# Four query products and four value-weight products of layer 1, held in written order on TensorE

## The chip, the cores and the metric

The kernel runs on one NeuronCore of a Trainium2 chip. Its time is the device time of one execution in microseconds (us). The kernel before took 3039.69 us as the median of 16 runs (3030.94 to 3050.21).

## The reference, cut to what matters

The reference is four transformer layers over 4 sequences of 512 tokens, 256 features each; every layer adds an attention-like part and a feed-forward part to `x`. Layer 1, where the change lies, is

```python
q = _rmsnorm(x @ wq_a, q_a_ln_w) @ wq_b            # 16 heads, 128 + 64 numbers each
q_nope, q_pe = q[..., :128], q[..., 128:]
ckv = x @ wkv_a
kv = _rmsnorm(ckv[..., :64], kv_a_ln_w) @ wkv_b    # per head: k_nope (128) and v (128)
q_pe, k_pe = _apply_rope(q_pe), _apply_rope(ckv[..., 64:])
scores = (q_nope @ k_nope.T + q_pe @ k_pe.T) * 192 ** -0.5     # causal
out = softmax(scores) @ v                          # all 16 heads side by side
x = x + out @ wo + _L1_ffn_ref(xn, ...)            # product-key experts and a gated unit
```

All of it is float32.

## The kernel before

**Absorbed weights.** The kernel never forms k_nope or v. Four times in layer 1, once for each group of four heads, `carry(g)` (L999 to L1022) multiplies the head's query weights by its key weights, `pw` (L1007) and `pw1` (L1015), and its value weights by its rows of `wo`, `pv` (L1008, the "value products"). ScalarE copies the results to SBUF (`wl0`, `wl1`, `wz`, L1019 to L1021). A value product has a stationary operand of 128 x 64, so it uses half of the columns of the array: heads 0 and 2 write partitions 0 to 63 of `pv`, heads 1 and 3 write partitions 64 to 127.

**Queries.** Heads go in pairs: 4 groups of heads, 4 sequences and 2 pairs make 32 pairs. For a pair, `queries(p)` (L1024 to L1046) makes two banks of 128 x 512 in PSUM, `pe` (the rotary part) and `pl` (the latent part). The contraction over 192 query latents is cut into 128 and 64, so each bank takes two matmuls: L1033 (`pe`, 128 rows), L1034 (`pl`, 128 rows), L1035 (`pe`, 64 rows: partitions 0 to 63) and L1036 (`pl`, 64 rows: partitions 64 to 127). In the text they are P0, L0, P1 and L1. P1 and L1 use different halves of the rows of the array. Every float32 matmul shows as two passes in the trace. Then ScalarE copies `pe` to `pes` (L1039), four SyncE DMAs swap 32-row blocks of it into `psw` (L1041), ScalarE scales `pl` into `qf` (L1043, L1044), and later VectorE rotates (`rotate`, L1048 to L1053) and writes the rest of `qf`.

**Heads.** The main loop (L1179 on) goes over 64 heads `s`. For each head, `probabilities(s, i)` for i = 0 to 3 makes the scores of query block i against keys 0 to 128(i+1) (L949, TensorE), adds the mask and takes the maximum (L952, VectorE), takes the exponential (L956, ScalarE), and, from i = 2 on, inverts the sums (L1067, VectorE) and multiplies by them (L1069, ScalarE: three tiles `pr0` to `pr2` after i = 2, the last, `pr3`, after i = 3). Beside it `turned(s - 1, j)` (L1071 to L1080) transposes column block j of the head before, 4 - j blocks of 128 x 128, on TensorE (L1076), and a copy of them to `PT` follows (L1080). Every second head, L1212 multiplies `PT` with the latents and L1226 with `wz`.

The next pair's queries are written after step i = 1 of every even head:

```python
            if i == 1 and s % 2 == 0 and s < 62:
                turning = queries(s // 2 + 1)
```

**What sets the order.** `weave` (L501) interleaves four streams of layer 1 by their costs: the attention, the product-key experts (L1236 on, mostly VectorE), a gated unit (L134, L212) and, at the end, the routing of layer 2. That gives the order in which instructions are *written*. The order in which they are *issued* is set afterwards: a scheduler at build time puts each engine's instructions in the order in which it reckons them ready, and keeps only true dependences. An engine then works through its list in that order. `tc.keep_in_program_order(ins)` adds one tie: `ins` is issued behind the instruction that was written just before it on the same engine, whichever stream that was. It adds no semaphore and no wait of its own; and something else may still be put between the two. The kernel before uses it in layer 1 for L1212, for L1051 and for the experts' dot products (L1340), not for the products of `queries` or `carry`.

Of the kernel before, what the change touches and what calls it, by code (L numbers as in the profile page):

```python
# [82 lines left out]
def v3(ap, b):  # L83
    return ap.rearrange("p (a b) -> p a b", b=b)
# [890 lines left out]
def latent_pieces(c, a, keep, open_pool):  # L975
# [4 lines left out]
    nc, tc = c.nc, c.tc  # L980
    QL, KL = 192, 64
# [3 lines left out]
    qa0 = c.tile(keep, [P, NT], "qa0")  # L985
    qa1 = c.tile(keep, [P, NT], "qa1")
# [12 lines left out]
    def carry(g):  # L999

        w = c.unit(a["l_units"][g])
        wqT, wkT, wvT = v3(w[:, :768], QL), v3(w[:, 768:1024], KL), v3(w[:, 1024:1280], KL)
        wo = v3(w[:, 1792:2816], DM)
        pw, pv = c.ps(), c.ps()
        for h in range(4):
            hk = slice(h * KL, (h + 1) * KL)
            nc.tensor.matmul(pw[:, hk], lhsT=wqT[:, h, :P], rhs=wkT[:, h, :], start=True, stop=True)  # L1007
            nc.tensor.matmul(  # L1008
                pv[(h % 2) * KL : (h % 2 + 1) * KL, (h // 2) * DM : (h // 2 + 1) * DM],
                lhsT=wvT[:, h, :], rhs=wo[:, h, :], start=True, stop=True,  # L1010
            )
        pw1 = c.ps()
        for h in range(4):
            hk = slice(h * KL, (h + 1) * KL)
            nc.tensor.matmul(pw1[KL:, hk], lhsT=wqT[:, h, P:], rhs=wkT[:, h, :], start=True, stop=True)  # L1015
        wl0 = c.tile(pool, [P, 256], "wl0")
        wl1 = c.tile(pool, [P, 256], "wl1")
        wz = c.tile(pool, [P, 2, DM], "wz")
        nc.scalar.copy(wl0, pw[:, :256])  # L1019
        nc.scalar.copy(wl1[KL:, :], pw1[KL:, :256])  # L1020
        nc.scalar.copy(wz, v3(pv, DM))  # L1021
        weights[g] = w[:, 1280:1536], w[:KL, 1536:1792], wl0, wl1, wz  # L1022

    def queries(p):  # L1024

        g, b, pair = p // 8, p // 2 % 4, p % 2
        if p % 8 == 0:
            carry(g)
        wpe0, wpe1, wl0, wl1, _ = weights[g]
        tokens = slice(b * SEQ, (b + 1) * SEQ)  # L1030
        cols = slice(pair * P, (pair + 1) * P)
        pe, pl = c.ps(), c.ps()
        nc.tensor.matmul(pe, lhsT=wpe0[:, cols], rhs=qa0[:, tokens], start=True, stop=False)  # L1033
        nc.tensor.matmul(pl, lhsT=wl0[:, cols], rhs=qa0[:, tokens], start=True, stop=False)  # L1034
        nc.tensor.matmul(pe, lhsT=wpe1[:, cols], rhs=qa1[:KL, tokens], start=False, stop=True)  # L1035
        nc.tensor.matmul(pl, lhsT=wl1[KL:, cols], rhs=qa1[KL:, tokens], start=False, stop=True)  # L1036

        pes, psw = (c.tile(pool, [P, SEQ], n, bufs=1) for n in ("pes", "psw"))
        nc.scalar.copy(pes, pe)  # L1039
        for to in range(0, P, 32):  # L1040
            nc.sync.dma_start(psw[to : to + 32, :], pes[to ^ 32 : (to ^ 32) + 32, :])  # L1041
        qf = c.tile(pool, [P, 2, SEQ], "qf")
        nc.scalar.mul(qf[:KL, 0, :], pl[:KL, :], -scale)  # L1043
        nc.scalar.mul(qf[KL:, 1, :], pl[KL:, :], -scale)  # L1044
        qfs[p] = qf
        return pes, psw, qf  # L1046
# [85 lines left out]
    for b in range(NB):  # L1132
        tokens = slice(b * SEQ, (b + 1) * SEQ)
        lats.append(latents(b))
        for t in range(TPB):
            tt = b * TPB + t
            pl = c.ps()[:, : QL + KL]
# [28 lines left out]
    finish(0)  # L1166
    yield 1.9
    turning = queries(0)
    yield 2.6
    finish(1)  # L1170
# [8 lines left out]
    for s in range(65):  # L1179
        if s < 64:  # L1180
            prs[s] = []
        for i in range(TPB):
            if s < 64:
                probabilities(s, i)
            if s > 0:
                if i == 0:
                    PTs[s - 1] = c.tile(pool, [P, 1280], "PT")
                ready, copy = copy, turned(s - 1, i)
                if ready:
                    ready()  # L1190
            if i == 0 and s % 2 == 1 and s < 63:
                rotate(*turning)
            yield 0.85
            if i == 1 and s % 2 == 0 and s < 62:
                turning = queries(s // 2 + 1)
                yield 2.6
# [13 lines left out]
        for j in range(TPB):  # L1210
            for h in range(2):
                tc.keep_in_program_order(nc.tensor.matmul(  # L1212
                    z[h * KL : (h + 1) * KL, j * P :], lhsT=cv[:, b * TPB + j, :],
                    rhs=PTs[s - 2 + h][:, START[j] : START[j] + SEQ - j * P],
                    start=(j == 0), stop=(j == TPB - 1),
# [4 lines left out]
        if pair == 1:  # L1220
            wz = weights[g][4]
            for t in range(0, TPB, 2):
                po = v3(c.ps("acc"), DM)
                for j in range(2):
                    for k in range(2):
                        nc.tensor.matmul(  # L1226
                            po[:, j, :], lhsT=zTs[k][:, (t + j) * P : (t + j + 1) * P],
                            rhs=wz[:, k, :], start=(k == 0), stop=(k == 1),
# [1078 lines left out]
```

## Time and profile before

| what | value |
|---|---|
| median of 16 runs | 3039.69 us |
| lowest, highest | 3030.94, 3050.21 us |
| the profiled execution: its own time | 3030.7 us |
| its span, first to last instruction | 3028.9 us |
| mean granted TensorE clock | 0.997 |
| TensorE busy | 2967.4 us (98% of the span) |
| VectorE, ScalarE, GpSimd busy | 2121.0 (70%), 1399.6 (46%), 915.6 us (30%) |

The profile is of one execution. "Busy" is the union of an engine's instructions; matmuls overlap in the pipeline and their ends are modelled, so what a matmul really takes of TensorE is read from the distance between the starts of two matmuls that follow each other. An "idle before" is only time in which no instruction of that engine ran. Layer 1's queries begin 836.5 us after the start of the span (first P0) and end at about 1444 us. The 16 runs lie in clusters: six at 3031, six at 3039 to 3041, four at 3044 to 3050; the profiled execution is one of the low ones.

### The profile page before, as it was taken

Reading aid. Unit: us, or ns where it says so; the run is one execution under the profiler, and the core shown is the slowest. Engines: PE = TensorE matmul, PEld = TensorE weight load, DVE = VectorE, ACT = ScalarE, POOL = GpSimd, SP = SyncE. Lnnn points to the kernel's source line nnn. Section 1 sums busy time; section 2 is a strip of 40 time slices with the busy share of each in tenths; the row PEclk is TensorE's granted clock in tenths of the full one; section 3 lists DMA queues with packets and bytes.
Section 4 is the critical chain, followed back from the end, with each engine's and each line's share of the span. In section 5 each row is a group of like instructions: output and inputs, shape, how many; then the busy total and the mean of one; then the engine's idle time right before and its main releaser. Section 6 shows DMA issues by size and latency. Waiting matters only on the chain.

```text
span 3028.9 us, 39747 instructions
## 1 busy us (share of the span) xinstructions
PE 2967.4 (98%) x13674; PEld 1957.4 (65%) x13674; DVE 2121.0 (70%) x5366; ACT 1399.6 (46%) x3336; POOL 915.6 (30%) x749
## 2 busy tenths in 40 slices
PE   8999999999999999999998999999999999999999
PEld 5666666566655555555676677777777756666666
DVE  5877878787777778787665767666666756666665
ACT  5444544444466666667524444444444433333332
POOL 0665555556210133332234200010010033333332
PEclk9999999999999999999999999999999999999999
DMA  3333333232221244444234000000000000000000
GB/s 134 94 108 123 98 97 117 83 124 84 88 69 37 64 120 105 104 104 123 83 105 127 16 1 29 1 22 8 1 21 1 22 1 22 22 22 22 22 1 29
DMA packets 89114, 185.39 MB, mean 61 GB/s; under 512 B 14192, under 2 KB 57216, under 8 KB 84176
## 3 DMA queue, kind: packets, MB, share of 16 engines
q1 hardware_dynamic: 74448, 135.05, 14.0%
q0 software_dynamic: 14176, 47.01, 6.6%
q8 instruction: 108, 1.77, 0.2%
q14 instruction: 94, 0.77, 0.1%
q10 hardware_dynamic: 288, 0.79, 0.1%
HBM read 160.92 MB, written 12.98 MB: 57 GB/s over the span
## 4 chain that ended last, share of the span: by engine, by line
PE 84%; DVE 8%; ACT 2%; DMA 2%; POOL 2%; issue 1%; SPq 0%; ACTq 0%; DVEq 0%; POOLq 0%
PE mm L301 19%; PE mm L134 14%; PE mm L949 7%; PE acc L301 6%; PE acc L1539 5%; PE acc L965 4%; PE tr L787 3%; PE tr L301 3%; PE tr L1531 2%; PE tr L1076 2%; PE mm L142 2%; PE tr L212 2%; PE acc L1212 2%; PE acc L765 2%; PE acc L212 2%; PE mm L1930 1%
## 5 line engine op out<-in xcount | busy, mean ns | idle before, releaser
L956 ACT ACTIVATE pr<-pr,nm 128x128 f32<-128x128 f32 (+3 forms) x512 | 286.3, 559 | 267.2 <-DVE nm L952 263.3
L312 ACT COPY part<-mm 128x256 f32<-128x256 f32 (+1 forms) x462 | 208.7, 459 | 232.1 <-PE mm L301 229.1
L301 PE MATMUL mm<-token_sums,unit_sums 128*128 128x512 f32 (+1 forms) x744 | 303.2, 490 | 0.0
L134 PE MATMUL mm<-xnT,wu 128*128 128x512 f32 x624 | 291.1, 604 | 3.8 <-DVE nm L952 3.7
L1330 POOL DMA_INDIRECT e<-in_p_experts,ids x128 | 128.9, 1007 | 478.0 <-DVE x L152 338.9
L952 DVE CUSTOM_DVE_ANT_0 pr<-mm,late 128x128 f32<-128x128 f32 (+3 forms) x512 | 245.6, 482 | 20.1 <-PE mm L949 17.3
L134 PE MATMUL mm<-xnT,w_in 128*128 128x512 f32 x512 | 229.2, 593 | 0.6 <-DVE cy L555 0.6
L461 DVE SCALAR_TENSOR_TENSOR x<-acc,cw,x 128x128 f32<-128x128 f32 x384 | 133.0, 347 | 112.4 <-PE acc L301 110.3
L134 PEld LDWEIGHTS mm<-xnT,wu 128*128 128x128 f32 x624 | 115.5, 192 | 125.4 <-issue 110.3
L555 DVE SCALAR_TENSOR_TENSOR cy<-mm,ws,cy 128x509 f32<-128x509 f32 (+2 forms) x216 | 160.2, 744 | 51.8 <-ACT cy L551 47.9
L949 PE MATMUL mm<-kf,qf 128*128 128x128 f32 (+3 forms) x512 | 176.0, 443 | 5.9 <-DVE qf L1053 4.5
L949 PE MATMUL mm<-k,q 128*128 128x128 f32 (+3 forms) x512 | 176.4, 434 | 1.1 <-DVE q L1478 1.0
L725 POOL TENSOR_TENSOR G<-G,CB 128x1024 f32<-128x1024 f32 x64 | 151.4, 2365 | 81.5 <-DVE G L688 75.4
L708 ACT ACTIVATE xD<-xc,ws 128x128 f32<-128x128 f32 x256 | 83.9, 391 | 191.7 <-POOL y L749 182.4
L301 PEld LDWEIGHTS acc<-down_sums,hidden_sums 128*128 128x128 f32 x768 | 114.8, 191 | 86.6 <-issue 83.4
L1532 DVE COPY PT<-tr 128x512 f32<-128x512 f32 (+3 forms) x256 | 124.7, 487 | 60.4 <-PE tr L1531 58.5
L134 PEld LDWEIGHTS mm<-xnT,w_in 128*128 128x128 f32 x512 | 96.5, 190 | 104.4 <-issue 94.4
L1539 PE MATMUL acc<-PT,V 128*128 128x512 f32 (+3 forms) x512 | 153.1, 442 | 7.3 <-DVE PT L1532 7.3
L688 DVE TENSOR_TENSOR_SCAN G<-G,eye 128x1024 f32<-128x1024 f32 x64 | 148.2, 2315 | 0.0
L1539 PEld LDWEIGHTS acc<-PT,V 128*128 128x128 f32 x512 | 93.3, 190 | 74.2 <-issue 30.6
L301 PE MATMUL mm<-xnT,wu 128*128 128x256 f32 (+1 forms) x368 | 137.0, 454 | 0.0
L444 DVE TENSOR_TENSOR whole<-mm,part 128x512 f32<-128x512 f32 x128 | 88.6, 692 | 68.2 <-PE mm L301 67.4
(408 smaller groups left out, 6713.9 us busy)
## 6 DMA issues: line engine op xcount, KB each, us to landing
G<-own SPq DMA_DIRECT2D x64, 512.0 KB, 4.4
w_in<-in_m_units SPq DMA_DIRECT2D x16, 1024.0 KB, 5.2
eb<-since SPq DMA_DIRECT2D x96, 128.0 KB, 3.3
wu<-in_o_units SPq DMA_DIRECT2D x8, 1536.0 KB, 6.5
wo<-in_m_units SPq DMA_DIRECT2D x16, 512.0 KB, 4.2
psw<-pes SPq DMA_DIRECT2D x128, 64.0 KB, 3.2
wu<-in_g_units SPq DMA_DIRECT2D x4, 1536.0 KB, 6.6
wu<-in_f_units SPq DMA_DIRECT2D x4, 1536.0 KB, 7.8
```

Source lines behind the costliest of these rows:

```text
L134: c.nc.tensor.matmul(out, lhsT=w[:, d, cols], rhs=c.xnT[:, d, tokens], start=(d == 0), stop=(d == 1))
L301: self.c.tc.keep_in_program_order(self.c.nc.tensor.matmul(bank, lhsT=lhsT, rhs=rhs, start=first, stop=True, skip_group_check=not first))
L312: self.c.nc.scalar.copy(r, bank)
L461: c.nc.vector.scalar_tensor_tensor(x, bank, self.factor(u, tt), x, ALU.mult, ALU.add)
L555: nc.vector.scalar_tensor_tensor(y[:, j:], src[:, : SEQ - j], conv[:, k, 3 - j : 4 - j], y[:, j:], ALU.mult, ALU.add,)
L688: tc.keep_in_program_order(nc.vector.tensor_tensor_scan(flat, flat, eye.rearrange("p h t -> p (h t)"), 0.0, ALU.mult, ALU.add))
L725: nc.gpsimd.tensor_mul(G, G, seqs[b][2][:, t, :][:, None, :].to_broadcast([P, HG, P]))
L949: kept(nc.tensor.matmul(sc, lhsT=q[:, i * P : n], rhs=k[:, :n], start=True, stop=True))
L952: nc.vector.tensor_tensor_reduce(out=pr, in0=sc, in1=late[:, SEQ - n :], scale=scale, scalar=-NEG, op0=ALU.add, op1=ALU.min, accum_out=nm,)
L956: nc.scalar.activation(pr, pr, AF.Exp, bias=nm, scale=-1.0, accum_out=total)
L1330: nc.gpsimd.indirect_dma_start(out=e, out_offset=None, in_=a["p_experts"], in_offset=bass.IndirectOffsetOnAxis(ap=ids[:, t, k : k + 1], ax ...
L1539: tc.keep_in_program_order(nc.tensor.matmul(z[:, j * P :], lhsT=head["V"][:, j, h, :], rhs=head["PT"][:, j, j * P :], start=(j == 0), stop ...
```

## The change

The four products of a pair and the four value products of a group are each passed through `keep_in_program_order`, and the value products get a loop of their own behind the loop of the query-key products. No instruction is added or taken away, and no size or operand is changed.

```diff
         for h in range(4):
             hk = slice(h * KL, (h + 1) * KL)
             nc.tensor.matmul(pw[:, hk], lhsT=wqT[:, h, :P], rhs=wkT[:, h, :], start=True, stop=True)
-            nc.tensor.matmul(
+        for h in range(4):
+            tc.keep_in_program_order(nc.tensor.matmul(
                 pv[(h % 2) * KL : (h % 2 + 1) * KL, (h // 2) * DM : (h // 2 + 1) * DM],
                 lhsT=wvT[:, h, :], rhs=wo[:, h, :], start=True, stop=True,
-            )
+            ))
...
-        nc.tensor.matmul(pe, lhsT=wpe0[:, cols], rhs=qa0[:, tokens], start=True, stop=False)
-        nc.tensor.matmul(pl, lhsT=wl0[:, cols], rhs=qa0[:, tokens], start=True, stop=False)
-        nc.tensor.matmul(pe, lhsT=wpe1[:, cols], rhs=qa1[:KL, tokens], start=False, stop=True)
-        nc.tensor.matmul(pl, lhsT=wl1[KL:, cols], rhs=qa1[KL:, tokens], start=False, stop=True)
+        kept, mm = tc.keep_in_program_order, nc.tensor.matmul
+        kept(mm(pe, lhsT=wpe0[:, cols], rhs=qa0[:, tokens], start=True, stop=False))
+        kept(mm(pl, lhsT=wl0[:, cols], rhs=qa0[:, tokens], start=True, stop=False))
+        kept(mm(pe, lhsT=wpe1[:, cols], rhs=qa1[:KL, tokens], start=False, stop=True))
+        kept(mm(pl, lhsT=wl1[KL:, cols], rhs=qa1[KL:, tokens], start=False, stop=True))
```

Lines behind the change stand one or two lines lower in the changed kernel (L1076 becomes L1078, L1033 to L1036 become L1035 to L1038 in written order).

## The prediction

> **What bounds the kernel.** I read the busy table and the chain of waits first. TensorE carries the end:
>
> ```profile
> PE 2967.4 (98%) x13674; PEld 1957.4 (65%) x13674; DVE 2121.0 (70%) x5366; ACT 1399.6 (46%) x3336; POOL 915.6 (30%) x749
> ...
> PE 84%; DVE 8%; ACT 2%; DMA 2%; POOL 2%; issue 1%; SPq 0%; ACTq 0%; DVEq 0%; POOLq 0%
> ```
>
> So time that TensorE gains or loses in layer 1 is, to first order, time of the kernel. Then TensorE's timeline at one group of products (group 4; I count the 32 pairs from 0). Columns: start, busy, line, number of passes.
>
> ```profile
> 906.15 1.02 PE L1033 MATMUL mm<-qa,wu 128*128 128x512 f32 x2
> 907.01 1.02 PE L1034 MATMUL mm<-qa,wl 128*128 128x512 f32 x2
> 907.99 0.84 PE L1076 MATMUL tr<-con,pr 128*128 128x128 f32 x3
> 908.76 1.12 PE L1035 MATMUL mm<-qa,wu 64*128 64x512 f32 x2
> 909.81 0.66 PE L1076 MATMUL tr<-con,pr 128*128 128x128 f32 x4
> 910.39 1.12 PE L1036 MATMUL mm<-qa,wl 64*128 64x512 f32 x2
> 911.45 1.13 PE L134 MATMUL mm<-xnT,wu 128*128 128x512 f32 x2
> ```
>
> Seven transposes of the head before (L1076) stand between the products. P1 (L1035) and L1 (L1036) take 1.05 us each (908.76 to 909.81). And here is a group that the scheduler left together (group 2):
>
> ```profile
> 871.65 1.02 PE L1033 MATMUL mm<-qa,wu 128*128 128x512 f32 x2
> 872.51 1.02 PE L1034 MATMUL mm<-qa,wl 128*128 128x512 f32 x2
> 873.46 0.69 PE L1035 MATMUL mm<-qa,wu 64*128 64x512 f32 x1
> 873.47 0.69 PE L1036 MATMUL mm<-qa,wl 64*128 64x512 f32 x1
> 874.00 0.59 PE L1035 MATMUL mm<-qa,wu 64*128 64x512 f32 x1
> 874.00 0.59 PE L1036 MATMUL mm<-qa,wl 64*128 64x512 f32 x1
> 874.52 0.91 PE L949 MATMUL mm<-kf,qf 128*128 128x384 f32 x2
> ```
>
> P1 and L1 start 0.007 us apart and run side by side: 1.06 us for both. The whole group takes 2.87 us.
>
> **What the change does to the order.** I compared the two programs' order on each engine. Before, P1 and L1 are neighbours in 13 of 32 groups, after it in 31 (not in group 0). But the tie reaches further: P0 is held behind whatever was written just before it, and that is the seven transposes. So in the changed program group 4 reads
>
> ```
> L1078 x7 (transposes), L1035 (P0), L1036 (L0), L1037 (P1), L1038 (L1)
> ```
>
> Seven transposes go ahead of the products, uncovered, in 15 of the 18 newly joined groups (3, 4, 5, 7, 12 to 15, 17, 18, 21, 23, 26, 29, 31). Outside layer 1 no engine's order changes.
>
> **Gain: sharing the array.** Group 15 is a split group with no visible wait: 4.83 us from P0 to the instruction after L1. Take off seven transposes at 0.109 us each (0.76, the distance of their starts) and 4.07 us are left, against 2.87: 1.20 us per group, of which 1.05 is the second 64-row product and 0.15 the slower starts around it. If nothing waited, 18 x 1.20 = 21.6 us. By the Trainium skill, "TensorE: Matmul & The Clock Gate", section "Measured speedup vs the span model", the second tile would cost only about 4 ns over the first; the rows show 0.53 us per shared pass, where a 128-row pass takes 0.43. By that rule a joined group would take 2.58 us, and the 18 would gain another 5 us; group 2 says no.
>
> **Gain: value products.** In groups of heads 1 and 3, L1007 and L1008 alternate; from 991.83 to 995.40 this takes 3.57 us. At 1146.00 two neighbouring L1008 products share the array: 0.58 us for both, where one alone takes 0.57. L1007 takes 0.22 us per head inside a run (start distances 0.11). New: 4 x 0.22 + 0.05 for the switch + 2 x 0.52 = 1.97, a gain of 1.6 us twice. Group of heads 2 has one shared pair already and group 0 is mixed with L1107's transposes; I take 0.8 for each (bounds 0 and 1.6). Together -4.8 us.
>
> **Loss: the transposes now wait uncovered.** This is the decisive step. What the seven transposes need comes from ScalarE:
>
> ```profile
> 906.83 0.72 ACT L956 ACTIVATE pr<-pr,nm 128x512 f32<-128x512 f32 x1 [0.35 <-DVE nm L952]
> 907.46 0.19 ACT L956 ACTIVATION_READ_ACCUMULATOR pr<-pr,nm 128x1 f32 x1
> 907.55 1.91 ACT L1069 ACTIVATE pr<-pr,total 128x128 f32<-128x128 f32 x4
> ```
>
> The four L1069 end at 907.94, 908.34, 908.85 and 909.46; the first transpose ran at 907.99, the second at 908.39, 0.05 us after their tile. TensorE was free at 906.15, and P0, L0 and P1 filled the time. ScalarE is not behind: it had idled 0.35 us for VectorE. This is the latency of score, mask, exponential, sum, scaling, and it won't move. In the changed order TensorE stands at 906.15 before a transpose that isn't ready until 907.99, and the last two can't run before 909.46 + 0.05. They end at 909.73 and the joined group at 912.60, against 911.45: **+1.15 us**, the 1.20 included.
>
> Generally: with R the end of the last L1069 after TensorE is free, the block takes R + 0.05 + 0.22 + 2.87. Over the 15 groups R is, in order, 3.00, 3.31, 3.06, 2.58, 3.94, 3.49, 2.94, 2.79, 3.38, 2.93, 2.57, 3.22, 3.04, 3.43, 2.21 (sum 45.9); the same instructions took 4.99, 5.30, 5.05, 4.97, 5.65, 5.77, 4.94, 4.83, 4.99, 4.92, 4.96, 4.99, 5.04, 4.89, 4.62 (sum 75.9). So 45.9 + 15 x 3.14 = 93.0 against 75.9: **+17.1 us**. The break-even is R = 5.06 - 3.14 = 1.9 us; the smallest is 2.21.
>
> The trace shows such a wait already. In group 6 the transposes stand ahead of the products, and no product passes them:
>
> ```profile
> 946.77 1.34 PE L1076 MATMUL tr<-con,pr 128*128 128x128 f32 x5 [0.70 <-ACT pr L1069]
> 948.29 0.44 PE L1076 MATMUL tr<-con,pr 128*128 128x128 f32 x2 [0.18 <-ACT pr L1069]
> ```
>
> Other groups, by the same reckoning: 16 (joined, transposes not moved) -1.15; 19 and 20 (L212 now covers the wait) -0.1 and -1.3; 10, 11 and 27 (joined before, now two or three transposes earlier) +1.4, +0.2, +0.4; 28 and 30 (layernorm's and seven other transposes go ahead) between 0 and +3.1 each, I take +1. Sum +1.5.
>
> **Who waits behind.** Behind a waiting transpose stand the products, then the next L949, whose scores VectorE (L952) waits for. `pe` of group 4 is complete at 912.60 instead of 909.81, so `pes`, the four SyncE DMAs (3.2 us to landing), `rotate` and `qf` come 2.8 us later, while their reader comes 1.15 later. VectorE's L1050 waits for `pes` with the experts' products queued behind it. TensorE's waits for `qf` are 4.5 us in three places now; if each grows by 1.6, +5. The other way, waits of up to 5 us on ScalarE and VectorE elsewhere can shrink while they catch up. I take +2 (-5 to +8). Moved SyncE issues (three) and one GpSimd copy: nothing, both queues are mostly empty.
>
> **Sum.** 17.1 + 1.5 - 4.8 + 2 = **+15.8 us**. On the profiled execution's own time, 3030.7, that is 3046.5. But that run is in the lowest of the clusters; the median stands 9.0 above it, so for a median I take 3039.7 + 15.8 = 3055.5, **3055 us**.
>
> **Rivals.**
> - *Nothing waits, faster.* If R fell below 1.9 us, blocks would shorten; at R under 0.5 the whole -21.6 - 4.8 = -26.4 us comes: 3013. For it: 98% busy, and the joined groups of before. Against it: R of 2.2 to 3.9 in all 15 groups, set by four L1069 in series. Chance 0.10.
> - *The wait is given back.* ScalarE and VectorE run ahead during each stop, and waits later in the pair vanish: the loss shrinks to within 6 us, 3034 to 3046. For it: VectorE is busy 79% between 940 and 1420 us (379.8 of 480), so it may profit. Against it: TensorE's listed waits in this stretch are only some 11 us. Chance 0.12.
> - *The stops also cost clock.* Between 1460 and 1480 us TensorE was busy 18.72 of 20 us, and the granted clock was 0.89: 2.2 us lost with 1.3 us idle. If a third of the 17 stops brought this, +12: 3068. "TensorE: Matmul & The Clock Gate", "Why this matters for your kernels", asks for no idle gap over about 3 us; gaps of under 2 us between transposes would cost nothing by it, but the row had less. Chance 0.10.
> - *Forecast*, +8 to +25 us: 0.68.
>
> **Range.** Low end: R shorter by 0.7 us in each block (-10.5) and the knock-on at -5 leave -2: 3037. High end: knock-on at +8 and groups 28 and 30 at their bound make +26, and a quarter of the stops losing clock brings 3074. Left out: the faster case and half of the clock case, near 0.16. What this kernel can tell from no change is 0.2%, 6.1 us: slower 0.78, same 0.12, faster 0.10.
>
> **What would show it.** In the new profile P1 and L1 start within 0.01 us of each other in 31 groups; L1078 (the transposes) shows idle time before it, released by ScalarE's scaling (now L1071), of some 15 x 2.5 = 38 us in place of 4.3; joined groups take 2.87 us; in layer 1 the span grows, before and behind it nothing moves. Wrong would be the step on R if those idle times stay under 1 us a group.

## The result and the profile after

The changed kernel takes 3094.69 us as the median of 11 runs (3087.93 to 3109.07), against 3040.65 us for the kernel before in the same comparison: ratio 1.0178 [1.0163, 1.0193], 54 us slower. The sign was forecast, the size was not: 3055 was predicted, and the range ended at 3074.

The profiled execution took 3090.85 us, 60.2 us more than that of before. First the busy table and the chain of waits of the changed kernel's page:

```profile
PE 2981.3 (97%) x13674; PEld 1959.9 (63%) x13674; DVE 2126.1 (69%) x5366; ACT 1398.7 (45%) x3336; POOL 912.9 (30%) x749
...
PE 80%; DVE 9%; ACT 4%; DMA 3%; POOL 2%; issue 1%; SPq 1%; DVEq 0%; ACTq 0%; POOLq 0%
```

TensorE has the same 13674 passes and is 14 us *more* busy, although products now share the array; ScalarE's part of the chain went from 2% to 4%. Where it lies is read by matching equal instructions of the two traces. Up to 836 us the changed kernel is 1.5 us late, at the last query product 56.7, at the end 60.2. So 55.9 of the 60.2 us lie between the first query product (P0) and the last (L1): this stretch takes 607.6 us before and 663.5 after. The windows over that stretch, before and then after (columns: window, its length, busy us of PE, PEld, DVE, ACT and POOL with their instructions, granted TensorE clock, DMA share, GB/s):

```profile
836.00:1445.00 609.00, 597.33 (x2627) 340.67 (x2626) 479.47 (x1657) 403.32 (x1066) 129.09 (x140) 1.00 0.36 90
```

```profile
836.00:1501.00 665.00, 608.86 (x2632) 342.40 (x2631) 484.93 (x1663) 402.74 (x1065) 128.03 (x143) 0.96 0.32 82
```

Two things are read off here. TensorE stood still for 609.00 - 597.33 = 11.7 us before and for 56.1 us after. And the granted clock fell from 1.00 to 0.96: the trace has 12 periods of half clock in this stretch, 51.2 us together, where before there was none.

Most of the idle time is the one that was predicted. The transposes' wait for the scaling in this stretch before (us in total, times, longest), and TensorE's waits after:

```profile
PE tr L1076 <- ACT pr L1069: 1.2, 4, 0.7
```

```profile
PE tr L1078 <- ACT pr L1071: 30.8, 30, 2.6
...
PE tr L1078 <- ACT xnT L126: 4.0, 4, 2.3
PE acc L1228 <- ACT zT L1220: 3.5, 4, 1.5
```

The same group 4 as in the prediction, now from the changed kernel:

```profile
909.56 0.82 PE L949 MATMUL mm<-kf,qf 128*128 128x128 f32 x4
912.06 1.34 PE L1078 MATMUL tr<-con,pr 128*128 128x128 f32 x5 [1.68 <-ACT pr L1071]
913.58 0.64 PE L1078 MATMUL tr<-con,pr 128*128 128x128 f32 x2 [0.17 <-ACT pr L1071]
914.02 1.92 PE L1035 MATMUL mm<-qa,wu 128*128 128x512 f32 x2
915.72 1.71 PE L1036 MATMUL mm<-qa,wl 128*128 128x512 f32 x2
917.36 0.69 PE L1037 MATMUL mm<-qa,wu 64*128 64x512 f32 x1
917.37 0.69 PE L1038 MATMUL mm<-qa,wl 64*128 64x512 f32 x1
```

Order, wait and neighbours are as written down beforehand: seven transposes first, TensorE waiting for ScalarE's scaling, then four products together, P1 and L1 0.007 us apart. But P0 and L0 now start 1.70 us apart, where they took 0.86. The windows around them show why:

```profile
910.30:913.70 3.40, 1.40 (x7) 0.66 (x7) 3.17 (x14) 3.05 (x10) 0.00 (x0) 1.00 0.00 0
913.70:917.10 3.40, 3.40 (x6) 1.33 (x6) 0.69 (x1) 1.07 (x5) 0.00 (x0) 0.50 0.08 10
```

In the stop TensorE is busy for 1.40 of 3.40 us at full clock; in the next 3.4 us it is always busy, at half clock. This is the mechanism to which the prediction gave one chance in ten.

### The profile page after: what moved, and what is told of

It is laid out like the page before. It is cut to its first block, busy times and chain, and to the rows that moved or that the text cites. A ratio compares the mean times of both kernels' runs of the same rounds, so it can differ in the third digit from the quotient of the medians.

```text
span 3089.1 us, 39736 instructions
## 1 busy us (share of the span) xinstructions
PE 2981.3 (97%) x13674; PEld 1959.9 (63%) x13674; DVE 2126.1 (69%) x5366; ACT 1398.7 (45%) x3336; POOL 912.9 (30%) x749
## 3 DMA queue, kind: packets, MB, share of 16 engines
q1 hardware_dynamic: 74448, 135.05, 13.7%
## 4 chain that ended last, share of the span: by engine, by line
PE 80%; DVE 9%; ACT 4%; DMA 3%; POOL 2%; issue 1%; SPq 1%; DVEq 0%; ACTq 0%; POOLq 0%
PE mm L301 19%; PE mm L134 13%; PE acc L301 6%; PE mm L949 6%; PE acc L1541 5%; PE acc L965 4%; PE tr L787 3%; PE tr L301 3%; PE tr L1533 2%; DMA psw<-pes 2%; PE mm L142 2%; PE tr L212 2%; PE acc L765 2%; DVE pr L952 1%; PE tr L1078 1%
## 5 line engine op out<-in xcount | busy, mean ns | idle before, releaser
L952 DVE CUSTOM_DVE_ANT_0 pr<-mm,late 128x128 f32<-128x128 f32 (+3 forms) x512 | 245.3, 482 | 14.3 <-PE mm L949 12.0
L461 DVE SCALAR_TENSOR_TENSOR x<-acc,cw,x 128x128 f32<-128x128 f32 x384 | 133.1, 347 | 112.6 <-PE acc L301 110.8
L1078 PE MATMUL tr<-con,pr 128*128 128x128 f32 x640 | 133.0, 294 | 41.1 <-ACT pr L1071 30.8
L1534 DVE COPY PT<-tr 128x512 f32<-128x512 f32 (+3 forms) x256 | 124.7, 488 | 62.0 <-PE tr L1533 60.2
L1078 PEld LDWEIGHTS tr<-con,pr 128*128 128x128 f32 x640 | 80.8, 145 | 114.7 <-ACT pr L1071 60.5
```

The source lines that it names most:

```text
L461: c.nc.vector.scalar_tensor_tensor(x, bank, self.factor(u, tt), x, ALU.mult, ALU.add)
L952: nc.vector.tensor_tensor_reduce(out=pr, in0=sc, in1=late[:, SEQ - n :], scale=scale, scalar=-NEG, op0=ALU.add, op1=ALU.min, accum_out=nm,)
L1078: nc.tensor.transpose(pt[:, (i - j) * P : (i - j + 1) * P], prs[s][i][:, j * P : (j + 1) * P], c.ident)
```

## The experiments

One theory and its rivals stood after the comparison. **Theory:** the tie of P0 puts the products behind transposes that are not ready; the stops cost their own length, and each stop costs clock afterwards. **Rivals:** the side-by-side products themselves lower the clock or cost time; or the value products or the ties as such do; or the loss beyond the predicted one is only waits of other instructions. Three chips were used, and each ratio below is to the kernel before on the same chip: its medians are 3036.39 us on the first chip (experiments 1 and 4, the first run of 5 and the first of 6), 3106.02 us on the second (2, the first run of 3, the second of 5 and the second of 6) and 3038.52 us on the third (the rest). The second chip was slower throughout: the kernel of experiment 3, which ran there and on the third, took 28 us longer there in layer 1's queries and some 54 behind them. So of that chip only ratios are compared.

**1. The value products alone** (`e1_values_only`): the kernel before with only the first part of the diff.

> Only the value products keep their own loop and their ties; the queries are as before. Theory (the loss of 54 us is made by the tie of the queries' first product behind the transposes): a small gain, 4 us, about 3037 us, since the carries of the changed kernel's profile are 0.9 to 1.4 us shorter each. Rival (the regrouped value products delay the first scores of a group): slower than before by more than 6 us.

Measured 3031.45 us, 0.9987 [0.9975, 1.0000]: -4.9 us by the medians, -3.9 by the ratio. In its trace the last query product comes 5.2 us earlier than before (both counted from the first group's), with steps of 1.7, 1.1 and 1.7 us at the three later groups of heads. The term -4.8 stands.

**2. The queries alone** (`e2_queries_only`): the changed kernel with the value products as before.

> The changed kernel with the value products left as they were before: only the four products of a pair are tied. Theory (the whole loss comes from the products held behind the transposes; the value products gain 5 us by themselves and have no part in it): 3037 + 58 + 5 - 5 or so, 3097 to 3101 us, and the listed wait of the transposes for ScalarE's scaling stays at 30 us. Rival (the value products' ties share in the loss): 3085 or less.

Measured 3147.34 us, 1.0147 [1.0120, 1.0173], and the transposes' wait for the scaling is 30.6 us, as expected. The time is a miss: on the first chip's scale the ratio is 3081 us, on the rival's side of its line, where 3097 to 3101 were expected. The whole change did not run on this slower chip, so the two ratios (1.0147 and 1.0178, whose intervals overlap) also compare chips, and by time this run settles nothing about the value products. That they have no part in the loss rests on experiment 1; that the queries alone bring the wait and a loss of some 1.5% is shown here.

**3. P0 without its tie** (`e3_first_free`, and once more as `e12_first_free_again`):

```diff
-        kept(mm(pe, lhsT=wpe0[:, cols], rhs=qa0[:, tokens], start=True, stop=False))
+        mm(pe, lhsT=wpe0[:, cols], rhs=qa0[:, tokens], start=True, stop=False)
```

> The changed kernel with three ties in place of four: L0, P1 and L1 are still tied, P0 (the first product) is not. TensorE's order then has P0 at its place of before, with seven transposes between the products again. Theory (the tie of P0 alone puts the products behind the transposes): 3031 to 3037 us, half clock in layer 1 under 15 us, the transposes' listed wait for the scaling under 3 us. Rival (any tie in queries costs, or the loss comes from P1 and L1 side by side): 3060 us or more.

> The kernel with three ties (P0 not tied) once more: in its first run all kernels on that chip stood longer behind layer 1, on transfers. TensorE's order in layer 1 is that of before but for the value products. Theory: 0.998 to 1.000 of the kernel before. Rival (the three ties cost something by themselves): 1.002 or more again.

Measured 1.0023 [1.0006, 1.0040] in the first run and 0.9980 [0.9962, 0.9997] in the second, whose stretch from first to last query product is 602.8 us, that of the value products alone (602.4). The first run's small loss (and 17.1 us at half clock, where under 15 were expected) did not come again; its chip is the likely cause, not shown. In the second run three ties of four cost nothing and gain next to nothing: P1 and L1 are neighbours in 15 groups (14 in the first run) in place of 13, and in group 4 of the second run the transposes stand between them as before.

```profile
912.57 0.84 PE L1078 MATMUL tr<-con,pr 128*128 128x128 f32 x3
913.33 1.12 PE L1037 MATMUL mm<-qa,wu 64*128 64x512 f32 x2
914.39 0.65 PE L1078 MATMUL tr<-con,pr 128*128 128x128 f32 x4
914.97 1.12 PE L1038 MATMUL mm<-qa,wl 64*128 64x512 f32 x2
```

A tie says "not earlier than", not "directly behind". What makes the four neighbours in the changed kernel is that P0 is held until all seven transposes are through and nothing is left to slip between.

**4. No sharing** (`e4_not_shared`): the changed kernel with the products written P0, P1, L0, L1, so that no two 64-row products follow each other.

> The changed kernel with the four products tied in the order P0, P1, L0, L1, so that the two 64-row products are never neighbours; all waits of the transposes stay. Theory (waits cost, sharing gains): sharing's gain is taken away, 31 groups x 1.24 us = +38 us on the changed kernel, about 3133 us, and the granted clock still falls in as many places. Rival (two products at once on the array are what lowers the clock or lengthens the groups): nearer to the kernel before, below 3070 us, with the clock at 1.0 in layer 1.

Measured 3120.08 us, 1.0267 [1.0234, 1.0300]. Group 4, from P0 to the instruction after L1:

```profile
911.75 1.02 PE L1035 MATMUL mm<-qa,wu 128*128 128x512 f32 x2
...
915.86 3.70 PE L134 MATMUL mm<-xnT,wu 128*128 128x512 f32 x8
```

That is 4.11 us against 2.87 for the shared products at full clock: 1.24 us, the 1.20 of the prediction. So sharing neither costs time nor lowers the clock; without it the change costs another 0.9%, some 27 us, where 38 were expected. Half clock in the stretch of the profiled run is 112.6 us, more than twice that of the changed kernel, but that run is the slowest of four (3130.47 us, mean granted clock 0.976). The other three have 0.981 to 0.986, the changed kernel's runs 0.982 to 0.988, so it is not shown that lone products lose more clock as a rule.

**5. The stops filled.** Extra 128x512 matmuls, tied ahead of the transposes; their result is overwritten by P0, so the output is the same and the kernel does more work. The same edit with three numbers of fills and two sets of groups:

```diff
+            if i == 0 and s % 2 == 0 and s // 2 + 1 in STOPS:   # STOPS: the 17 groups with a stop
+                early = c.ps()
+                for k in range(3):                              # 3, 2 or 1
+                    tc.keep_in_program_order(nc.tensor.matmul(
+                        early, lhsT=qa0[:, :P], rhs=qa0[:, :SEQ], start=True, stop=True))
...
-                turning = queries(s // 2 + 1)
+                turning = queries(s // 2 + 1, early)            # pe = early
```

First three fills in all 31 groups that the loop writes (`e6_filled`):

> The changed kernel with three extra 128 x 512 matmuls per pair (into the bank of pe, overwritten by P0; work that the reference does not need) tied ahead of the waiting transposes, where TensorE stood idle: some 30 x 2.6 = 78 us more TensorE work. Theory (half of the loss is the clock, which is halved for 3.4 us after a stop: 51 us at half clock in layer 1): the clock stays at 1.0 and the kernel gets faster than the changed one in spite of the work, about 3073 us. Rival (the clock's fall does not come from the stops, or costs little because TensorE was waiting anyway): no gain, 3095 us or, with the added work on the path, up to 3170 us.

Measured 3104.24 us, 1.0211 [1.0181, 1.0241]: a miss in time. The causes it was to remove are gone: half clock in the stretch is 13.7 us, the transposes' wait 3.5. The count was wrong: only 17 groups have a stop to fill, and in the other 14 each 2.57 us is plain work, 36 us. The next run, on the second chip, left those out (`e8_filled_stops`):

> The changed kernel with three 128x512 matmuls added ahead of the transposes, whose result is overwritten, as in the run with fills in all pairs, but only in the 17 groups in which the changed kernel has a stop (3, 4, 5, 7, 12 to 15, 17, 18, 21, 23, 26, 28 to 31); it computes the same output. Theory (a fill of 2.57 us costs nothing where TensorE stood still, and brings back the clock; in the other groups it is 2.57 us more work each): 3104 - 14 x 2.57 = 3068, between 3062 and 3076, half clock in layer 1 under 25 us. Rival (the stops cost no clock, the fill adds its own time; or the added ties are the cost): 3090 or more.

Measured 1.0098 [1.0069, 1.0126], +30 us (+31.5 was expected); half clock 13.7 us. By the ratios, adding 17 x 2.57 = 43.7 us of matmuls to the changed kernel makes it *faster*, by 0.8%. To separate stop and clock, one and two fills, which fit inside the stops, beside the changed kernel on the same chip (`e9_one_fill`, `e10_two_fills`, `e11_changed_again`):

> The changed kernel with one extra 128x512 matmul (0.86 us; its result is overwritten, the output is the same) ahead of the transposes in the 17 groups with a stop; in 15 of them it comes just ahead of the last score and the seven transposes. There it takes the place of idle time, so that without any effect on the clock the time would not move: +0 to +3 us against the changed kernel (two of the 17 fills do not lie in front of the stop). Theory (the stops also cost clock, some 25 us in all): a stop shorter by 0.86 us gives back a part of it, -5 to -20 us against the changed kernel, half clock in layer 1 between 15 and 45 us. Rival (the rest of the loss is waits of others, not clock): within 3 us of the changed kernel.

> The same with two extra matmuls (1.72 us) in each of the 17 groups. They still fit into the stops (R of 2.2 to 3.9 us), so without an effect on the clock the time is that of the changed kernel, +3 us or so for the two groups in which the fill lies elsewhere. Theory: the stops left are under 1.5 us, nearly all of the clock comes back: -15 to -28 us against the changed kernel, half clock in layer 1 under 20 us. Rival: within 5 us of the changed kernel.

> The changed kernel once more, as the measure for the runs with one and two fills on the same chip. Expected: 1.016 to 1.019 of the kernel before; its half clock in layer 1 is 40 to 65 us again, if that comes from the stops and not from chance.

| kernel | us | ratio to before | half clock in the stretch | transposes' wait for scaling, whole kernel |
|---|---|---|---|---|
| the change again | 3087.03 | 1.0160 [1.0143, 1.0177] | 64.9 us | 30.1 us |
| one fill | 3073.02 | 1.0113 [1.0086, 1.0140] | 13.7 us | 18.4 us |
| two fills | 3069.10 | 1.0107 [1.0086, 1.0128] | 6.8 us | 10.1 us |

A fill does not move the transposes, which still wait for ScalarE; it only makes TensorE busy in that time: the block of group 4 is 1.2 us longer than before with one fill and with two, where the prediction said +1.15 and the changed kernel has +2.90. Yet one fill saves 14 us and two save 18. All runs show it, not only the profiled ones: the mean granted clock is 0.985 to 0.986 in the four runs of the change, 0.991 to 0.995 with one fill and 0.992 to 0.996 with two. The half clock with one fill is below the 15 to 45 us that were expected. The same group 4 with one fill:

```profile
913.36 1.34 PE L1078 MATMUL tr<-con,pr 128*128 128x128 f32 x5 [0.82 <-ACT pr L1071]
...
915.15 1.02 PE L1035 MATMUL mm<-qa,wu 128*128 128x512 f32 x2
916.01 1.02 PE L1036 MATMUL mm<-qa,wl 128*128 128x512 f32 x2
```

and its windows:

```profile
911.40:914.80 3.40, 2.35 (x9) 0.92 (x7) 3.33 (x15) 3.04 (x10) 0.00 (x0) 1.00 0.00 0
914.80:918.20 3.40, 3.32 (x11) 1.33 (x12) 0.75 (x2) 1.33 (x7) 0.00 (x0) 1.00 0.08 10
```

Busy for 2.35 us in place of 1.40, still waiting for ScalarE, and the products behind it run at full clock, 0.86 us apart. The rival (only waits) falls: it expected these runs within 3 and 5 us of the changed kernel.

**6. The queries written earlier** (`e5_ahead`): the changed kernel with the next pair's queries written ahead of the transposes they would otherwise wait behind; and the same move in the kernel before, without any tie (`e7_ahead_free`).

```diff
+            if i == 0 and s % 2 == 0 and s < 62:
+                turning = queries(s // 2 + 1)
             if s > 0:
                 if i == 0:
                     PTs[s - 1] = c.tile(pool, [P, 1280], "PT")
                 ready, copy = copy, turned(s - 1, i)
...
             if i == 1 and s % 2 == 0 and s < 62:
-                turning = queries(s // 2 + 1)
                 yield 2.6
```

> The changed kernel with one thing moved: a pair's queries are written one step earlier, ahead of the transposes that they were tied behind. 28 of 32 groups share the array, and the transposes stand behind the products. Theory: 15 more shared groups than before x 1.2 us and 4 us from the value products, no stop, so 22 us faster than before, about 3018 us, with the clock at 1.0 between 836 and 1440 us. Rival (sharing costs): not faster than 3040 us.

> The kernel before, without any tie, with only the place changed at which the next pair's queries are written: right behind the scores of query block 0 and ahead of the transposes of the head before, in place of behind the scores of block 1. P1 and L1 become neighbours in 24 of 32 groups. Theory (what decides is whether the products stand ahead of the transposes and next to each other, not the tie): about 3011 (the run with the same place and all ties) + 5 for the value products + 5 x 1.2 for the pairs left apart = 3022, between 3016 and 3028. Rival (the ties themselves are what gains in that run): 3034 to 3040.

Measured 3011.13 us, 0.9921 [0.9899, 0.9943], for the first: faster than both kernels, 25 us below before. The second: 0.9948 [0.9932, 0.9963], 16 us below. Group 4 of the first:

```profile
904.34 1.02 PE L1035 MATMUL mm<-qa,wu 128*128 128x512 f32 x2
905.20 1.02 PE L1036 MATMUL mm<-qa,wl 128*128 128x512 f32 x2
906.15 0.69 PE L1037 MATMUL mm<-qa,wu 64*128 64x512 f32 x1
906.16 0.69 PE L1038 MATMUL mm<-qa,wl 64*128 64x512 f32 x1
```

The four products are together and stand *in front of* the seven transposes, so they cover ScalarE's latency themselves: in the first run the transposes' wait for the scaling is 1.7 us in the stretch, half clock 3.4 us. The gain of the prediction's first rival (26.4 us if nothing waited) is there after all; the change had only put the products on the wrong side of the wait. The first run is 7 us faster than expected, which is not explained. Without ties the value products are as before (5 us) and 7 of the 32 groups are apart in its trace in place of 5 (1.2 us each; 8 and 4 were expected). The gain is 9 us smaller, on another chip, so the place makes most of it and the ties the smaller part.

## Why the prediction was wrong in size

**Right, and measured so.**
- *The order and R.* R sums to 48.6 us over the 15 blocks, after 45.9; group 21 alone makes 1.7 of the difference. The transposes' idle time is 41.1 us in the whole kernel; "of some 15 x 2.5 = 38 us" was forecast.
- *The block.* In the 8 blocks that contain no half clock (3, 5, 12, 14, 15, 17, 26, 31) the formula R + 3.14 gives +9.4 us in all; measured +10.2. A joined group takes 2.87 us in all of them.
- *The value products,* -4.8: measured -4.9 [-7.6, 0].

**Wrong.** By matched instructions the 60.2 us divide as follows; the row on the rest is what is left over.

| term | predicted | measured |
|---|---|---|
| 8 blocks without half clock | +9.4 | +10.2 |
| 7 blocks with half clock (4, 7, 13, 18, 21, 23, 29) | +7.7 | +21.6 |
| groups 28 and 30 | +2 | +14.3 |
| groups 10, 11, 16, 19, 20, 27 | -0.5 | -1.8 |
| value products (from the run with them alone) | -4.8 | -4.9 |
| rest of the stretch: "Who waits behind" | +2 | +16.5 |
| ahead of and behind the stretch | 0 | +4.3 |
| sum | +15.8 | +60.2 |

The step that failed is the third rival, *the stops also cost clock*: it was left out of the sum, at 0.10, and priced at "+12" if a third of the 17 stops brought it. In the trace 7 of the 15 blocks and both of groups 28 and 30 ran partly at half clock. How much of the loss this is, the run with two fills shows, in which none of these 17 blocks contains half clock: the 15 grow by 20.0 us in place of 31.8, and groups 28 and 30 by 6.3 (the two fills there, which do not lie in front of the stop and cost 2 x 1.72 = 3.4 us, taken off) in place of 14.3. That is 20 us of clock in the blocks. The whole stretch from first to last query product is 607.6 us before, 663.5 and 663.8 in the two profiles of the change, and 640.9 with two fills, 3.4 of them those fills: 26 us went with the clock. In the medians it is 18 + 3.4 = 21 us. Not all of the 26 can be the clock itself: 51.2 us at half clock hold at most 25.6 us, and with two fills 6.8 us of it are left, so at least some 4 us are waits that shrank with it.

The row used beforehand, 18.72 us busy of 20 at clock 0.89, had already shown half clock behind little idle time, and the prediction still put the term at nothing. What was missed is how short a stop suffices, and that the forecast's own 2.5 us of waiting in one place was such a stop.

By the Trainium skill, "TensorE: Matmul & The Clock Gate", section "Why this matters for your kernels", it is idle gaps over about 3 us that bring the throttled clock back. Here the longest gap in front of a transpose was 2.6 us and that of group 4 was 1.68 us, and half clock followed: by the rule the clock would have cost nothing, the runs say some 21 us. The measurement decides.

Second, *groups 28 and 30* were given +1 each between 0 and +3.1. Without half clock (two fills, their own 1.72 us taken off) they lost 2.7 and 3.5 us: about the upper bound. The timeline of group 28 after the change:

```profile
1419.31 1.65 PE L121 MATMUL tr<-con,xn 128*128 128x128 f32 x8 [1.20 <-DVE xn L110]
1421.19 0.33 PE L1078 MATMUL tr<-con,pr 128*128 128x128 f32 x1 [0.24 <-ACT xnT L126]
1422.87 1.66 PE L1078 MATMUL tr<-con,pr 128*128 128x128 f32 x5 [1.35 <-ACT xnT L126]
1424.84 0.69 PE L1078 MATMUL tr<-con,pr 128*128 128x128 f32 x2 [0.31 <-ACT pr L1071]
```

Before, P0 and L0 stood between layernorm's transposes (L121) and covered their waits, and the waits for a `tr` bank that ScalarE has still to empty (L126). Now 3.10 us of waiting stand in a row ahead of P0, which starts at 1425.32 and runs at half clock.

Third, the *knock-on* was +2 with an upper bound of +8. Nearly without the clock it is some 10 us: the 33.3 us by which the stretch grows with two fills, less 3.4 of fills, 6.3 of groups 28 and 30 and 20.0 of the blocks, plus 1.8 and 4.9 of gains. (The 6.8 us at half clock left in that run can hold at most 3.4 of it.) Of single waits that grew, that of `wz`'s products (L1228) for `zT` went from 0.4 us before to 3.1 with two fills; the rest is spread over many groups and was not followed to its causes. This part stays open.

One reading beside the sum was also wrong. The 2.58 us that the prediction sets against a joined group's 2.87 take 0.43 us, a 128-row pass, for each shared pass. But a 64-row pass takes 0.53 us when alone, too (1.05 us for the two of P1), and its neighbour starts 0.007 us later: sharing adds next to nothing to the pass, and group 2 does not speak against the rule cited there.

The rivals *nothing waits* and *the wait is given back* fell with R: hardly anything was given back. Apart from the value products and groups 16, 19 and 20, the delay shrinks by 0.6 us behind group 6 and by some 2 us behind the last query product.

## What to carry to other kernels

An ordering tie is only as good as the instruction it ties to: if that one waits for a slow engine, everything tied behind it waits too, and work that had covered the latency comes after it. Put independent matmuls in front of the waiting instruction, not behind it: the same four products, the same ties, moved by one step in the program, turned 1.8% slower into 0.8% faster. And when TensorE is 98% busy, count a new stop twice, once for its length and once for the clock that may fall behind it.

## What the runs showed of the hardware

- The granted clock is decided in pieces of 3.413 us: in a trace the periods of half clock begin on one grid (913.7, 958.1 and 978.5 us are 13 and 6 pieces apart) and last one, two or more pieces. The Trainium skill, "TensorE: Matmul & The Clock Gate", section "What's actually happening", tells of a free-running window of 4096 cycles, about 3.4 us, and the grid agrees. Cut by it, the periods of half clock in the two profiles of the changed kernel follow pieces in which TensorE was busy for 0.78 to 2.19 us (25 of 27 periods; two follow a full piece). Other pieces with 1.52 to 2.2 us did not lead to one; below 1.5 all did. (Over all 14 traces, from 830 to 3000 us, every piece at full clock with under 1.4 us busy led to one. Above that both occur; some follow pieces of 2.8 us or more, the row at 1475.5 us of the kernel before among them, so the busy time of one piece is not the whole rule.) So the same stop costs clock or not by where it falls on the grid: ahead of group 3, a wait of 1.31 us for `qf` and one of 0.69 us before a transpose fell into two pieces (2.10 and 2.19 us busy) in the first profile of the change, and no half clock followed; in the second profile both fell into one piece (1.63 us busy), and 6.8 us at half clock followed.
- A stop shortened by one matmul of 0.86 us brought half clock in the stretch from 64.9 to 13.7 us.
- Two 64-row products in different halves of the rows take 0.53 us per shared pass, and a 64-row pass alone takes 0.53 us too, where a 128-row pass takes 0.43 (group 4 without sharing: 4.11 us for four products).
